# Handing a sum over states back from TensorE to GpSimd, and a new order of the first turns

## The chip, the cores and the metric

The kernel runs on one core of a Trainium2 chip. The metric is device time in microseconds (us) of one execution. The engines that matter are TensorE (PE, matmuls and transposes), VectorE (DVE), ScalarE (ACT), GpSimd (POOL) and SyncE (SP, which here only issues loads). Each engine runs its own instructions strictly in the order in which the program lists them; an instruction that has to wait for another engine holds up everything behind it on its own engine.

## The reference

A layer in the manner of Mamba, with a feed-forward part, and then a dense mixture of 8 experts. Tokens are x of shape (16, 256, 128): 16 sequences of 256 tokens, width 128, all in fp32. Cut to what matters:

```python
def layer(x):                         # one sequence after another, width 128
    xi, z = split(layernorm(x) @ in_proj_w.T)       # 256 inner channels each
    xc = silu(causal_conv(xi, 4 taps) + conv_b)
    dt, B, C = split(xc @ x_proj_w.T)               # 8, 16 and 16 columns
    dt = softplus(dt @ dt_proj_w.T + dt_proj_b)
    dA  = exp(dt * A)                               # for each of 16 states
    dBx = dt * B * xc
    h_t = dA_t * h_(t-1) + dBx_t                    # the scan over time
    y   = sum over the 16 states of h * C           # the "sum over states"
    y   = (y + D * xc) * silu(z)
    x   = x + y @ out_proj_w.T
    return x + relu(layernorm(x) @ w1.T + b1) @ w2.T + b2

x = layernorm(x + layer(x))
acc = 0
for e in range(8):                                  # every token through every expert
    acc += (silu(x @ Wg[e]) * (x @ Wu[e])) @ Wd[e]  # 128 -> 512 -> 128
out = layernorm(x + acc)
```

## The kernel before

The 16 sequences are cut into 8 groups of two, so a group has 512 tokens. Activations lie with channels on the 128 partitions and the 512 tokens along the row; the 256 inner channels are two halves. A group passes through these stages:

- `stage_a`: the loaded tokens `xt` (L209) are normalised (statistics `st_a` on DVE, L274; `rs`, `nb` on GpSimd, L283; four activations to `xh` on ScalarE, L291), transposed on PE (`pxn`, L298), scaled to `xn`, projected (`pi`), convolved (`hc`, `xc`), projected again (`pd`, `dbc`) and written to DRAM as `bc`, so that rows of B and C can be loaded back spread over all partitions. `dt` and `u` = dt * xc follow. `stage_gate` makes the gate `zg`.
- The scan. The 16 states of two halves make 32 steps per group (the text calls each of them a state; k counts them, so `hC_10` is step 10). Step k takes four to five instructions: `dA` = exp on ScalarE into one of three PSUM banks (L474, "decay"), `dBx` = B * u on GpSimd (L486, "inject"), the scan along time on DVE (L494), its product with C, `hC` (L497, on DVE, or on GpSimd where the scan wrote to SBUF, `hS`), and the addition to the running sum over states, `add_state`: `y` += `hC` on GpSimd (L523), or a matmul of `hC` with the identity into a PSUM bank `py` that PE keeps adding to (L521). Where a group's sum is on PE, the last step also adds `y` with a matmul (L527), and the product with the gate, `yt` (L536), runs on DVE; without it, `yt` runs on GpSimd.
- `stage_c`: `po` (16 matmuls out of `yt`, L551), `x1` on DVE, its norm (`st_b`, `ve_b` on DVE, `rs_b`, `nb_b` on GpSimd), `res` on GpSimd, `x1h`, `ph`, `h2`, four `pf` with their `r`, `pff`, `res` on DVE (L612), its norm (`ve_c`, `rs_c`), `x2` on ScalarE, the transposes `px` (L298 again) and the copy `x2T`, which feeds the experts.
- The experts: 32 slices a group (8 experts of 4 parts). A slice is `up` (`pg`, L641, and its Silu `h` on ScalarE, L643), `across` (`pu`, L650, and the product `h` = pu * h on DVE, L651) and `down` (`acc`, L667).
- `stage_e`: `ao`, `pao`, the last norm and the store.

Memory that sets the order: four rotating PSUM banks (`grab`, `give`, `take`) serve `pg`, `pu`, `py` and all the transposes and projections; B and C tiles of 512 KB hold four states each and have two buffers each, so the load of `B_12` (states 12 to 15) can't begin before the last `dBx` of `B_4` (`dBx_7`) has read it. All loads (tokens at L209, B and C at L463, expert weights at L251 to L253) go through SP's queue in program order.

The order of the instructions is written out by hand as strings of one-letter words. `PRE` is run once before the turns, `START` has one string for each of the first 18 turns, `TURN` has eight strings that repeat until the end. Each word does one thing if it can, and otherwise nothing:

- `d`, `i`, `s`, `a`: the next decay, inject, scan step, `add_state`; `p` is `s` with the product on GpSimd, `e` is `a` with the sum on PE
- `u`, `x`, `w`: the next up, across, down; `L`: loads of B and C whose conditions are met
- `A` (with `B`, `G`), `C`, `Z`: half a stage of `stage_a` (of convolutions, of gates), `stage_c`, `stage_e`; `P` prepares A
- `m` (`busy`): four transposes of the identity, filler, only while there are no experts; `S`, `E`: whether Silu and softplus may run now

The experts of group 0 begin once its `x2T` is there; until then PE has the filler, the projections and the sums. The tokens of group g+1 are asked for (`load_x`) at the top of a turn, and the turn's loads of B and C follow. In `add_state`, the condition on `on_pe` lets a group's first half of states start a sum on PE if more than two banks are free; once begun, any `e` goes on with it, and its bank is held until `yt`.

Of the kernel before, what the change touches and what calls it, by code (L numbers as in the profile page):

```python
# [12 lines left out]
P = 128  # L13
L = 256
DM = 128
NH = 2
NS = 16
# [15 lines left out]
NLATE = 4  # L33
# [15 lines left out]


PRE = (
# [4 lines left out]
)  # L56
START = (
# [44 lines left out]
)  # L102
TURN = (
# [26 lines left out]
def kernel(  # L130
# [25 lines left out]
    nc = tc.nc  # L156
# [15 lines left out]
    def bank(tag, name, bufs=1, w=TB):  # L172
        return ps.tile([P, TB], FP, tag=tag, bufs=bufs, name=name)[:, :w]


    free = list(range(NB))
    owner = {}

    def grab(name, w=TB):
        owner[name] = free.pop(0)  # L180
        return bank(f"b{owner[name]}", name, w=w)

    def give(name):
        free.append(owner.pop(name))
# [4 lines left out]
    def wides(tag, name, bufs, n, w):  # L189
        t = act.tile([P, n * TB], FP, tag=tag, bufs=bufs, name=name)  # L190
        return t[:, : n * w].rearrange("p (n w) -> p n w", n=n)
# [21 lines left out]
    ident = const.tile([P, P], FP, tag="ident", name="ident")  # L213
# [103 lines left out]
    def launch(kind, stage):  # L317

        next(stage)
        running[kind].append(stage)  # L320
# [178 lines left out]
    def sums(g, h):  # L499

        n = 1 if NH * W[g] <= TB else NH
        c = h * W[g] if n == 1 else 0
        return f"py{g}_{h if n > 1 else 0}", slice(c, c + W[g])

    def add_state(t, on_pe):

        g, k = scans[t]
        s = state[g]
        n, h = divmod(k, NH)
        hC = s.pop(("hC", k))  # L510
        y = s["y", h]
        last = n == NS - 1
        name, cols = sums(g, h)
        if on_pe and not (name in owner or (n < NS // 2 and len(free) > 2)):
            on_pe = False
        if on_pe or (last and ("sum", h) in s):
            first = name not in owner
            if first:
                s["py", name] = grab(name)
            s["sum", h] = s["py", name][:, cols]  # L520
            nc.tensor.matmul(s["sum", h], lhsT=ident, rhs=hC, start=first, stop=False, skip_group_check=True)  # L521
        else:
            nc.gpsimd.tensor_tensor(y, y, hC, ALU.add)  # L523
        if last:
            assert s["gated"] >= h
            if ("sum", h) in s:
                nc.tensor.matmul(  # L527
                    s["sum", h], lhsT=ident, rhs=y, start=False,
                    stop=h == NH - 1 or sums(g, NH - 1)[0] != name, skip_group_check=True,
                )  # L530
                y = s["sum", h]
            if h == 0:
                s["yt"] = wides("yt", f"yt{g}", 1, NH, W[g])

            engine = nc.vector if y is not s["y", h] else nc.gpsimd
            engine.tensor_tensor(s["yt"][:, h, :], y, s["zg"][:, h, :], ALU.mult)  # L536
            if name in owner and (h == NH - 1 or sums(g, NH - 1)[0] != name):
                give(name)
            if h == NH - 1:
                launch("C", stage_c(g))  # L540
# [91 lines left out]
    def parts(g, j):  # L632

        n = TB // W[g]
        return [divmod(j * n + i, NF) + (slice(i * W[g], (i + 1) * W[g]),) for i in range(n)]
# [18 lines left out]
    def down(g, j):  # L654
        s = state[g]
        if j == 0:

            n = NTAIL if g == NG - 1 else 1
            s["acc"] = [bank("dA" if i else "acc", f"acc{g}_{i}", ND if i else 1, W[g] // n) for i in range(n)]
        last = g == NG - 1  # L660
        late = last and j >= NJ[g] - NLATE
        if late and j < NJ[g] - 1:
            return
        todo = [p + (s.pop(("h", i)),) for i in range(j - NLATE + 1 if late else j, j + 1) for p in parts(g, i)]
        for part, acc in enumerate(s["acc"]):
            for e, f, cols, h in todo:
                nc.tensor.matmul(  # L667
                    acc, lhsT=wd[:, e, f, :], rhs=h[:, cols][:, bass.ts(part, acc.shape[1])],
                    start=(e == 0 and f == 0), stop=(e == NE - 1 and f == NF - 1),
                )  # L670
# [55 lines left out]
    def add_next(on_pe=False):  # L726
        g, k = scans[min(at["a"], len(scans) - 1)]
        if at["a"] < at["s"] and (
            k // NH < NS - 1 or state[g].get("gated", -1) >= k % NH and not running["C"]
        ):  # L730
            add_state(at["a"], on_pe)
            at["a"] += 1

    def step_next(pool=False):
        t = at["s"]
        if ready(t) and t < at["a"] + BUFS:
            if at["d"] == t:
                decay_next()
            if at["i"] == t:
                inject_next()  # L740
            if at["C"] * NL <= t:
                load_next("C")
            if min(at["d"], at["i"], at["C"] * NL) > t:
                step(t, pool)
                at["s"] += 1
# [21 lines left out]
    def silu(on):  # L767
        silus[0] = on or not experts

    def busy():  # L770
# [8 lines left out]
        L=loads, s=step_next, a=add_next, i=inject_next, d=decay_next, u=rise, x=cross, w=lower,  # L779
        S=lambda: silu(True), E=lambda: silu(False), m=busy,  # L780
        p=lambda: step_next(True), e=lambda: add_next(True),
# [10 lines left out]
    while at["w"] < sum(NJ) or any(running.values()):  # L792
# [3 lines left out]
        g, k = scans[min(at["a"], len(scans) - 1)]  # L796
# [56 lines left out]
```

## Time and profile before

| | us |
|---|---|
| Median of 3 runs | 934.35 (933.2 to 934.37) |
| The profiled execution's own time | 933.03 |
| Its span, first to last instruction | 930.9 |
| Busy in it: PE | 882.6 (95%) |
| DVE | 712.4 (77%) |
| ACT | 711.9 (76%) |
| POOL | 718.8 (77%) |

The mean granted TensorE clock is 0.979 of full speed. By stretches of the span, busy us of each engine, the granted clock, and the share of the DMA engines in use:

| Stretch | PE | DVE | ACT | POOL | Clock | DMA |
|---|---|---|---|---|---|---|
| 0 to 40 | 27.8 | 19.2 | 27.9 | 15.8 | 0.91 | 0.68 |
| 40 to 80 | 30.2 | 38.3 | 20.0 | 37.3 | 0.83 | 0.60 |
| 80 to 120 | 33.2 | 35.7 | 21.1 | 38.3 | 0.91 | 0.39 |
| 120 to 160 | 34.9 | 21.7 | 33.6 | 38.3 | 0.91 | 0.20 |
| 160 to 200 | 40.0 | 28.2 | 34.1 | 36.2 | 1.00 | 0.27 |
| 200 to 300 | 98.1 | 84.2 | 90.6 | 92.3 | 1.00 | 0.25 |
| 300 to 700 | 395.9 | 354.6 | 359.7 | 355.6 | 1.00 | 0.26 |

Mean durations of the large groups of instructions:

| Instruction | Line | ns | Count |
|---|---|---|---|
| `dBx` on POOL | L486 | 1275 | 256 |
| `y` on POOL | L523 | 1275 | 223 |
| `hC` on POOL | L497 | 1271 | 27 |
| scan on DVE | L494 | 1221 | 229 |
| `hC` on DVE | L497 | 691 | 229 |
| `h` product on DVE | L651 | 684 | 256 |
| `dA` on ACT | L474 | 685 | 256 |
| Silu `h` on ACT | L643 | 597 | 256 |
| table load on ACT | L474, L643 | 1283 | 91 and 90 |
| sum on PE | L521 | 695 | 66 rows |

How to read it: a PE, DVE, ACT or POOL row of the profile gives start and duration in us, engine, source line, operation, and out<-in; what stands in square brackets behind it is the idle time of the engine just before and what ended it. An fp32 matmul of 128x512 shows as two rows, so 33 sums are 66 rows. SPq is SP's DMA queue, and its rows are the moments at which a load is issued. A load of `xt` (256 KB) lands 4.4 us after its issue by the median of the eight.

### The profile page before, as it was taken

To read this page: it belongs to the slowest core of one execution; us is meant where nothing else is said; L and a number is where in the kernel's file an instruction comes from. 1 tells how busy PE (TensorE), PEld (TensorE's weight loads), DVE (VectorE), ACT (ScalarE), POOL (GpSimd) and SP (SyncE) were. 2 spreads that over 40 slices of the span, in tenths; PEclk is the share of its full clock that TensorE was granted. 3 is DMA by queue.
4 is the path that set the end of the run, shared out by engine and by line. 5 is a ranking of instruction groups with operands and counts; after the bars stand their busy time and mean duration, and the time that the engine had idled before them with its cause. 6 is when DMAs were issued, how large, how long until landed. Compare 5 with 4: busy or idle time off the path is not lost. (4 is left out here: it accounts for less than half of the span.)

```text
span 930.9 us, 8897 instructions
## 1 busy us (share of the span) xinstructions
PE 882.6 (95%) x2520; PEld 424.5 (46%) x2520; DVE 712.4 (77%) x1142; ACT 711.9 (76%) x996; POOL 718.8 (77%) x639
## 2 busy tenths in 40 slices
PE   6778797999999999999999999999999999999996
PEld 2334543445444543445344543454444544455564
DVE  4599865676989889988988998988898899723222
ACT  5834588888899799989898889979998889533222
POOL 1799998998999897999799879999799979700000
PEclk9888899999999999999999999999999999999998
DMA  7573411131233221223322223221322222000000
GB/s 203 199 236 137 134 62 68 68 103 57 82 102 110 83 90 60 91 90 102 94 79 90 80 94 101 92 96 53 103 90 92 91 79 90 1 1 11 1 0 12
DMA packets 38129, 79.76 MB, mean 86 GB/s; under 512 B 5936, under 2 KB 19136, under 8 KB 38080
## 3 DMA queue, kind: packets, MB, share of 16 engines
q1 hardware_dynamic: 33456, 76.58, 24.7%
q10 hardware_dynamic: 4624, 2.62, 1.0%
q8 instruction: 20, 0.33, 0.1%
q14 instruction: 29, 0.24, 0.1%
HBM read 76.57 MB, written 2.62 MB: 85 GB/s over the span
## 5 line engine op out<-in xcount | busy, mean ns | idle before, releaser
L486 POOL TENSOR_TENSOR dBx<-B,u 128x512 f32<-128x512 f32 x256 | 320.5, 1275 | 0.0
L494 DVE TENSOR_TENSOR_SCAN dA<-dA,dBx 128x512 f32<-128x512 f32 x229 | 279.7, 1221 | 17.0 <-ACT dA L474 14.0
L523 POOL TENSOR_TENSOR y<-y,hC 128x512 f32<-128x512 f32 x223 | 279.4, 1275 | 0.7 <-DVE hC L497 0.4
L641 PE MATMUL pg<-x2T,wg 128*128 128x512 f32 x512 | 255.7, 601 | 7.3 <-ACT h L643 4.8
L650 PE MATMUL pu<-x2T,wu 128*128 128x512 f32 x512 | 250.8, 595 | 3.3 <-ACT h L643 3.3
L651 DVE TENSOR_TENSOR h<-pu,h 128x512 f32<-128x512 f32 x256 | 170.9, 684 | 107.8 <-PE pu L650 104.8
L667 PE MATMUL acc<-h,wd 128*128 128x512 f32 (+1 forms) x576 | 251.4, 546 | 0.1
L643 ACT ACTIVATE h<-pg 128x512 f32<-128x512 f32 x256 | 147.1, 597 | 114.5 <-PE pg L641 112.4
L474 ACT ACTIVATE dA<-dt,A 128x512 f32<-128x512 f32 x256 | 169.4, 685 | 39.7 <-DVE hC L497 34.3
L497 DVE TENSOR_TENSOR hC<-dA,C 128x512 f32<-128x512 f32 x229 | 158.3, 691 | 18.0 <-POOL y L523 3.5
L667 PEld LDWEIGHTS acc<-h,wd 128*128 128x128 f32 x576 | 107.7, 191 | 110.2 <-issue 100.8
L650 PEld LDWEIGHTS pu<-x2T,wu 128*128 128x128 f32 x512 | 95.7, 190 | 123.0 <-issue 89.9
L641 PEld LDWEIGHTS pg<-x2T,wg 128*128 128x128 f32 x512 | 94.5, 191 | 123.2 <-issue 83.4
L474 ACT ACT_TABLE_LOAD x91 | 116.8, 1283 | 2.4 <-ACT x L291 0.5
L643 ACT ACT_TABLE_LOAD x90 | 115.5, 1283 | 3.3 <-ACT dbc L377 1.8
L283 POOL TENSOR_TENSOR rs_e<-ve_e,mhalf 128x4 f32<-128x4 f32 (+1 forms) x9 | 8.5, 945 | 123.4 <-DVE ve_e L281 123.4
L521 PE MATMUL py<-hC,ident 128*128 128x512 f32 x66 | 39.0, 695 | 9.8 <-DVE hC L497 6.0
L402 POOL TENSOR_TENSOR u<-dt,xc 128x512 f32<-128x512 f32 x15 | 19.5, 1302 | 30.0 <-ACT dt L397 30.0
L494 DVE TENSOR_TENSOR_SCAN hS<-dA,dBx 128x512 f32<-128x512 f32 x27 | 32.3, 1211 | 11.5 <-POOL hC L497 6.5
L443 DVE SCALAR_TENSOR_TENSOR hc<-pi,cw,hc 128x510 f32<-128x510 f32 (+2 forms) x48 | 35.5, 744 | 5.2 <-ACT hc L436 4.1
L497 POOL TENSOR_TENSOR hC<-hS,C 128x512 f32<-128x512 f32 x27 | 34.2, 1271 | 5.4 <-issue 3.2
L585 PEld LDWEIGHTS pff<-w,r 128*128 128x128 f32 x256 | 31.7, 194 | 9.4 <-issue 6.6
(90 smaller groups left out, 612.9 us busy)
## 6 DMA issues: line engine op xcount, KB each, us to landing
B<-bc SPq DMA_DIRECT2D x64, 512.0 KB, 3.8
C<-bc SPq DMA_DIRECT2D x64, 512.0 KB, 4.5
xt<-in_x_dram SPq DMA_DIRECT2D x8, 256.0 KB, 4.4
wg<-in_Wg_dram SPq DMA_DIRECT2D x8, 256.0 KB, 5.1
wu<-in_Wu_dram SPq DMA_DIRECT2D x8, 256.0 KB, 5.4
wd<-in_Wd_dram SPq DMA_DIRECT2D x8, 256.0 KB, 5.9
out_dram<-x ACTq DMA_DIRECT2D x7, 256.0 KB, 4.2
bc<-dbc ACTq DMA_DIRECT2D x8, 64.0 KB, 2.2
```

Source lines behind the costliest of these rows:

```text
L443: nc.vector.scalar_tensor_tensor(hv[:, :, k:], pv[:, :, : L - k], cw[:, h, KC - 1 - k : KC - k], hv[:, :, k:], ALU.mult, ALU.add,)
L474: nc.scalar.activation(s["dA", k], s["dt"][:, h, :], AF.Exp, scale=A_sb[:, h, n : n + 1])
L486: nc.gpsimd.tensor_tensor(s["dBx", k], s["B", k // NL][:, n % NC, :], s["u"][:, h, :], ALU.mult)
L494: nc.vector.tensor_tensor_scan(to, dA, s.pop(("dBx", k)), 0.0, ALU.mult, ALU.add)
L497: engine.tensor_tensor(hC, to, s["C", k // NL][:, k // NH % NC, :], ALU.mult)
L521: nc.tensor.matmul(s["sum", h], lhsT=ident, rhs=hC, start=first, stop=False, skip_group_check=True)
L523: nc.gpsimd.tensor_tensor(y, y, hC, ALU.add)
L641: nc.tensor.matmul(pg[:, cols], lhsT=wg[:, e, bass.ts(f, P)], rhs=s["x2T"], start=True, stop=True)
L643: nc.scalar.activation(s["h", j], pg, AF.Silu)
L650: nc.tensor.matmul(pu[:, cols], lhsT=wu[:, e, bass.ts(f, P)], rhs=s["x2T"], start=True, stop=True)
L651: nc.vector.tensor_mul(s["h", j], pu, s["h", j])
L667: nc.tensor.matmul(acc, lhsT=wd[:, e, f, :], rhs=h[:, cols][:, bass.ts(part, acc.shape[1])], start=(e == 0 and f == 0), stop=(e == NE - 1 ...
```

## The change

Three things are edited.

In `add_state`, a sum that a group has begun on PE may now be handed back. If the next `add_state` of the same half is called without PE (`a`, not `e`), it is not the last state, the group is not group 0 and the group's bank is held, then PE adds the running `y` to the bank with one more matmul against the identity, ScalarE copies the bank to `y`, the bank is given back, and the state itself is added on GpSimd as usual. `s["own", h]` notes it, and keeps that half from starting a sum on PE again. In the program that results, PE sums two of group 1's 32 states, `hC_1` and `hC_10`, and hands each back at once. Over the whole program PE's own sums of states (L521) go from 33 to 29, the matmuls of `y` at the last state from 3 to 2, and two matmuls and two copies are new; of the `hC` products, 17 are on GpSimd and 239 on DVE, where it was 27 and 229; the sums `y` on GpSimd are 227 for 223, `yt` 14 for 13.

In `down`, the products `h` are read and no longer removed from the table of names; the instructions are the same.

All the words of `PRE` and `START` are new (the strings of 18 turns, below only their beginnings); `TURN` stays. With them, among the loads on SP, the tokens of group 3 stand behind the load of `B_12` of group 2, where they stood before it.

```diff
 PRE = (
-    "L A B A G A L B A G B A A B G m G G A P L L B A A B B L B B "
...
+    "d B A G A B A B A B L A A B A G P B G B A L G P P i B A B A "
...
 )
 START = (
-    "C i C L L Z m e e a L d C Z p s C s A Z m L s m A s Z i s i "
-    "s e",
...
+    "A A L a s s C s A d C s s s p m a L L e Z e",
...
 )
...
         name, cols = sums(g, h)
-        if on_pe and not (name in owner or (n < NS // 2 and len(free) > 2)):
+        if on_pe and not (name in owner or (n < NS // 2 and len(free) > 2 and ("own", h) not in s)):
             on_pe = False
+        if not on_pe and not last and g > 0 and name in owner:
+
+            nc.tensor.matmul(s["sum", h], lhsT=ident, rhs=y, start=False, stop=True, skip_group_check=True)
+            nc.scalar.copy(y, s.pop(("sum", h)))
+            s["own", h] = True
+            give(name)
         if on_pe or (last and ("sum", h) in s):
...
-        todo = [p + (s.pop(("h", i)),) for i in range(j - NLATE + 1 if late else j, j + 1) for p in parts(g, i)]
+        some = range(j - NLATE + 1 if late else j, j + 1)
+        todo = [p + (s["h", i],) for i in some for p in parts(g, i)]
```

86 rows, old and new, of tables (PRE, START) are left out of this document.

## The prediction

> **What bounds the kernel now.** I read the page's engine shares and slices first, then PE's waits, then single engines in order of time around the second group.
>
> ```profile
> PE 882.6 (95%) x2520; PEld 424.5 (46%) x2520; DVE 712.4 (77%) x1142; ACT 711.9 (76%) x996; POOL 718.8 (77%) x639
> ...
> PE   6778797999999999999999999999999999999996
> ...
> POOL 1799998998999897999799879999799979700000
> ```
>
> PE (second row, 23.3 us a slice) is full from slice 7 on; before that it mostly runs filler (`busy`). So the time is: the start of the experts, the PE work behind it, and PE's waits there. GpSimd is as full as PE in slices 1 to 34; while the second group (group 1) is scanned, both bind.
>
> ```profile
> 121.61 2.99 PE L641 MATMUL pg<-x2T,wg 128*128 128x512 f32 x4
> ...
> 200.36 2.28 PE L551 MATMUL po<-outw,yt 128*128 128x128 f32 x16
> ...
> 227.84 0.60 PE L298 MATMUL px<-ident,x 128*128 128x128 f32 x4
> ```
>
> Experts start at 121.61; `po` of group 1 starts at 200.36, its `px` (the transposes whose copy is the next experts' input) at 227.84. From 121.6 to 200.4 PE has 81 matmuls of 128x512 at 0.86 (two rows each; four rows stand 1.72 apart), 69.7, in 78.8 us: 9.1 lost. From 200.4 to 227.8 it loses nothing.
>
> ```profile
> 199.49 1.27 POOL L536 TENSOR_TENSOR yt<-y,zg 128x512 f32<-128x512 f32 x1
> ...
> 204.91 1.02 POOL L283 TENSOR_TENSOR rs_b<-ve_b,mhalf 128x4 f32<-128x4 f32 x1 [0.47 <-DVE ve_b L281]
> ...
> 220.83 1.01 POOL L283 TENSOR_TENSOR rs_c<-ve_c,mhalf 128x4 f32<-128x4 f32 x1 [3.30 <-DVE ve_c L281]
> ```
>
> GpSimd finishes group 1's `yt` at 200.76, just as PE comes to `po`. Behind it lies slack: GpSimd waits 3.30, and DVE 5.90:
>
> ```profile
> 211.18 0.85 DVE L274 BATCH_NORM_STATS2 st_a<-xt 128x6 f32<-128x128 f32 x4
> ...
> 218.60 0.69 DVE L612 TENSOR_TENSOR res<-pff,res 128x512 f32<-128x512 f32 x1 [5.90 <-PE pff L585]
> ...
> 196.94 0.43 SPq L209 DMA_DIRECT2D xt<-in_x_dram x1
> ...
> 215.07 0.32 SPq L463 DMA_DIRECT2D B<-bc  x1
> ```
>
> The last two rows: group 3's tokens are asked for at 196.94, long before `st_a` reads them, and before the load of group 2's `B_12` at 215.07, which has to wait until GpSimd has read `B_4` for the last time (`dBx_7`).
>
> **The change, part by part.** Times are in us of the span; "order" is that of the changed program's instructions on each engine. Pitches, from rows that stand back to back in time: GpSimd 1.24 (five `dBx` in 6.16, nine in 11.10), a state on DVE (scan and `hC`) 1.93 (60.39, 62.32, 64.24), a scan alone 1.15 (two in 2.33), an `h` product 0.64 (two in 1.28), a matmul 0.86, a table load and the activation behind it 1.29 (137.94 to 139.23).
>
> *The handover.* Of group 1's 32 states two pass over PE (`hC_1`, `hC_10`), each followed by one matmul of `y` and one ScalarE copy out of PSUM: 4 x 0.86 on PE, of which two lie before the experts, beside filler. Before, 7 of group 1's sum matmuls lay behind the start of the experts, now 2: 5 x 0.86 = 4.3 of PE work leaves. The copy does not occur in the trace; the nearest rows, `x2T` (0.578) and `ao` (0.585), bound it; 0.58, hidden once behind `dA_11` and once between two Silus. The other edit (`s["h", i]` read, not popped) issues the same instructions: nothing.
>
> *GpSimd and DVE over the whole kernel.* `hC` on GpSimd 27 to 17, `y` 223 to 227, `yt` 13 to 14: -5 x 1.24 there; DVE takes ten `hC` more at 0.69 and loses one `yt`. One table load fewer on ScalarE, -1.28 (its row on the page).
>
> [...]
>
> *Start of the scan.* Group 1's four normalising activations (1.63) now stand ahead of group 0's `xn`, which covers a wait of 0.57: +1.0. A gate (0.6) and `dt` of group 1 (0.67), less one gate activation, stand ahead of the first decay: first scan at 35.2 for 33.1, +2.1.
>
> *Group 0.* Up to the second `yt`, DVE now has 27 states of 1.93 (scan and `hC`) and 6 scans of 1.15, where it had 28 and 5; with two `yt` of 0.64: 60.3 for 60.8. Then two states instead of one stand on DVE ahead of `x1`: `x1` at 99.3 for 95.8, +3.5. From there to the first expert it was 25.8; the `r` activations are less interrupted, and `x2T` now waits behind two `hc`: 24.9. Experts start at 124.2, +2.6.
>
> *Group 1's scan.* GpSimd from its first `dBx` to group 1's last `yt` has 134 instructions for 137: 158.9 busy for 162.7. Before, it idled 8.8 on the way (2.18, 0.44, 0.52, 0.68, 0.65, 0.44, 3.17, 0.72). The 3.17 goes back to PE, which had three banks left with `py` held and waited twice for a Silu (2.28 and 2.42); now the bank is back after one matmul. I take 4.9 idle: from 32.1 the last `yt` ends at 195.9, against 200.8. PE is there at 194.3 and has lost less than before. So far the change is 4.8 ahead.
>
> *From `po` to `px`: where it goes.* DVE had 3 scans and 4 `h` products between `ve_b` and `res`; now it has 7 states (5 x 1.93, 2 x 1.14), 7 products (0.64) and group 3's statistics (2.1): 18.5 without a gap, where it took 13.9 with 5.9 of slack. `ve_b` ends at 199.8, `res` at 218.4 at best, against 218.6: nearly all the lead is gone. PE, in order, now has `pxn` in front of `pg_30`, behind `xh`, behind four decays (three banks), the last of which waits for DVE's scan 7: `px` at 227.2 at best.
>
> *The queue.* In SP's order the load of `xt` for group 3 now stands behind that of `B_12`. `B_12` waits for `dBx_7` on GpSimd, the sixth instruction of 1.24 behind `rs_b`/`nb_b` (199.9 to 201.1): 208.5. `xt` is asked for at 208.85 and lands 3.0 to 5.8 later, median 4.4: 213.2. DVE comes to `st_a` at 199.8 + 0.62 + 1.93 + 4 x 0.62 + 2 x 1.93 = 208.7 and stands 4.5 (3.1 to 5.9). That this is a real wait the trace shows at the first groups, where the load stands behind `C_8`:
>
> ```profile
> 101.34 0.43 SPq L209 DMA_DIRECT2D xt<-in_x_dram  x1
> ...
> 105.75 0.87 DVE L274 BATCH_NORM_STATS2 st_a<-xt 128x6 f32<-128x128 f32 x4 [2.97 <-DMA xt<-in_x_dram]
> ```
>
> Queued behind `st_a` on DVE are scans 4 to 7 and `res`; behind those, ScalarE's `dA_7` to `dA_10`, two Silus, `xh`; behind `xh`, PE's `pxn`. PE is at `pxn` at 219.0 and can go on at 227.0: 8 idle. `px` then stands at 232.4, +4.6.
>
> *The clock.* After a gap of that length PE starts slow. Nearest rows:
>
> ```profile
> 99.90 1.63 PE L298 MATMUL ph<-ident,x1h 128*128 128x128 f32 x4 [4.14 <-ACT x1h L291]
> ...
> 102.39 3.78 PE L595 MATMUL pf<-h,w 128*128 128x512 f32 x4
> ...
> 153.70 1.43 PE L650 MATMUL pu<-x2T,wu 128*128 128x512 f32 x2 [2.42 <-ACT h L643]
> ```
>
> After 4.14 idle four rows took 3.78 (1.88 warm) and the transposes 1.0 more; after 2.42 two rows took 0.4 more. Between 0.4 and 2.9; I take 2.0, nearer the long gap.
>
> *Behind `px`.* `pxn` already lies in front: -0.4. Matmuls left are the same (after `px` 31/29/28 of up, across and down are done; before 31/30/27). DVE and GpSimd have 9 instructions fewer each until group 2's `px`; the waits of before between 230 and 290 (0.70 + 0.34 + 0.34 + 0.17 + 0.28 = 1.8) may shrink: -1.2, between -1.8 and 0. From there both programs repeat the same turns.
>
> Sum: +4.6 + 2.0 - 0.4 - 1.2 = **+5.0**. The profiled execution took 933.03 (span 930.9 and 2.1 around it), the median of the runs is 934.35: 938.0 and 939.4; I say 938.7.
>
> **Rivals.**
> *The load is hidden after all* (not slower). `st_a` waits less if DVE is late itself or GpSimd passes `dBx_7` early; for it, DVE's stretch is 18.5 of unbroken work. Then `px` comes at 227.2: -0.6 - 0.4 - 1.2 = -2.2, and some 0.7 for hops between engines that I left out: 932.5. Against it: both times hang on the same `ve_b`, so lateness moves them together; it decides only if the load stands under 1 us.
> In this case PE idles 3.5 at `pxn`, between the two clock rows. [...]
>
> *The lead at `po` is kept* (not slower). If PE's fewer matmuls and the earlier `yt` carry through, -4.8 + 0.9 (one product fewer was done by `po`) - 0.4 = -4.3: 930.0. For it: PE's 9.1 of loss in group 1's scan. Against it: DVE's 18.5.
>
> *GpSimd slips too* (slower). My walk leaves GpSimd 0.3 to 1.1 of margin at `hC_17`, `hC_24` and `hC_28` behind DVE's scans; a wait there like the old 3.17, ScalarE's 13 table pairs being in series with it, adds 3 to 4.5 on top: 942.
>
> *It does not do what it says*: two states of 32 on PE is hardly a sum begun there; the order decides. That is in the forecast.
>
> **How the numbers follow.** Forecast (slower by 2 to 7) 0.50; with GpSimd slipping 0.14; load hidden 0.22; lead kept 0.14. A measurement tells about 0.2% (1.9 us) from no change. Faster: the last case and a third of the hidden one, 0.20. Same: the rest of that and the forecast's low edge, 0.16. Slower 0.64. The forecast's own range is 935.5 to 941.5 (stall 3.1 to 5.9, clock 0.4 to 2.9). The range over cases: 931 to 943.5.
>
> **What would show it.** In the changed profile: first scan near 35, `pg` at 124, group 1's `yt` near 196; SP's `xt` some 0.4 behind `B_12`; DVE waiting 3 to 6 at `st_a` for a DMA; PE waiting about 8 at `pxn` for `xh`, with a lower clock behind it; `px` near 234. I am wrong if `st_a` finds its data, or if `yt` of group 1 ends after 199.

## The result and the profile after

The changed kernel takes 939.83 us (median of 3 runs, 939.39 to 939.96) where the kernel before took 934.35; the ratio is 1.0062, 95% interval 1.0039 to 1.0084. It is slower by 5.5 us; 938.7 was forecast. Later, beside the experiments, the same kernel took 941.31 against 933.48 (1.0075, 1.0062 to 1.0088). The profiled execution took 939.96, its span is 938.2 (930.9 before).

From the page of the changed kernel: the engines' busy times, and the slices of PE, GpSimd and PE's granted clock.

```profile
PE 873.5 (93%) x2514; PEld 417.0 (44%) x2514; DVE 717.6 (76%) x1151; ACT 709.6 (76%) x997; POOL 713.4 (76%) x634
...
PE   6577789987999999999999999999999999999996
...
POOL 1699999996799878999699969998799979700000
PEclk9799999998999999999999999999999999999998
```

PE is busy for 9 us less and GpSimd for 5 less, in a longer span. PE's row has an 8 and a 7 in the ninth and tenth slice (188 to 235 us), where the kernel before had nines, and its clock is 8 in the tenth. That place in time, from the timelines of the engines (start, duration, engine, line, what is written out of what; in brackets the idle time before and what ended it):

```profile
122.24 1.12 PE L642 MATMUL pg<-x2T,wg 128*128 128x512 f32 x2 [1.65 <-ACT x2T L626]
...
193.20 1.26 POOL L537 TENSOR_TENSOR yt<-y,zg 128x512 f32<-128x512 f32 x1
...
194.52 2.64 PE L552 MATMUL po<-outw,yt 128*128 128x128 f32 x14 [2.31 <-POOL yt L537]
...
199.43 1.02 POOL L278 TENSOR_TENSOR rs_b<-ve_b,mhalf 128x4 f32<-128x4 f32 x1 [1.29 <-DVE ve_b L276]
...
208.62 0.43 SPq L204 DMA_DIRECT2D xt<-in_x_dram  x1
...
213.75 0.88 DVE L269 BATCH_NORM_STATS2 st_a<-xt 128x6 f32<-128x128 f32 x4 [4.76 <-DMA xt<-in_x_dram]
...
217.08 0.69 ACT L469 ACTIVATE dA<-dt,A 128x512 f32<-128x512 f32 x1 [3.06 <-DVE hC L492]
...
222.25 0.68 DVE L613 TENSOR_TENSOR res<-pff,res 128x512 f32<-128x512 f32 x1
...
224.75 1.64 ACT L286 ACTIVATE xh<-xt,nb_a,rs_a 128x128 f32<-128x128 f32 x4
225.30 1.62 PE L293 MATMUL pxn<-ident,xh 128*128 128x128 f32 x4 [3.50 <-ACT xh L286]
226.71 1.92 PE L642 MATMUL pg<-x2T,wg 128*128 128x512 f32 x2
228.42 1.55 PE L669 MATMUL acc<-h,wd 128*128 128x512 f32 x2
...
232.38 0.60 PE L293 MATMUL px<-ident,x 128*128 128x128 f32 x4
```

Group 1's `yt` ends at 194.46, 6.3 earlier than before. Then the tokens of group 3 are asked for at 208.62, behind `B_12`; DVE stands 4.76 for them; the decays behind its scans are late (3.06); `xh` stands behind the decays, and PE stands 3.50 for `xh`. The two matmuls behind it take 1.71 at a clock of 0.50 and 1.38 at 0.62 to the next start, where one at 1.00 takes 0.86. `px` is 4.5 later than before. A comparison that stopped here would seem to have the whole result. It would be wrong, as the starts of `px` in all groups show:

| Start of `px`, group | 0 | 1 | 2 | 3 | 4 | 5 | 6 | 7 | end of span |
|---|---|---|---|---|---|---|---|---|---|
| Before | 119.30 | 227.84 | 330.77 | 433.26 | 535.17 | 637.08 | 738.99 | 832.39 | 930.9 |
| After | 119.49 | 232.38 | 331.35 | 434.42 | 537.19 | 640.32 | 742.99 | 837.02 | 938.2 |
| Difference | 0.19 | 4.54 | 0.58 | 1.16 | 2.02 | 3.24 | 4.00 | 4.63 | 7.3 |

The 4.5 shrink to 0.6 by group 2, and then grow by 0.6 to 1.2 in each group of turns whose strings were not changed. Counted from the word lists: when the repeating turns begin (turn 18), the kernel before has begun 32, 30 and 28 slices of the experts (up, across, down), the changed one 31, 29 and 27. (It is also one `dBx` and one sum ahead there; e2 below keeps that lead and has the pace of before.) The profiles agree: at `px` of group 2 PE has run 63, 62 and 59 before, 62, 61 and 58 after, and one less in every later group too. One slice is three matmuls, 3 x 0.86 = 2.6 us of PE. So of the 4.54, 2.6 are gone by group 2 only because that work is still to be done, and the remaining 1.4 are gained on the way; the slice is paid at the end (4.63 to 7.3). The new cost is the 4.05 between group 2 and group 7.

GpSimd's timeline in group 4 shows where it comes from. Before:

```profile
449.68 1.28 POOL L486 TENSOR_TENSOR dBx<-B,u 128x512 f32<-128x512 f32 x1
456.12 1.02 POOL L283 TENSOR_TENSOR rs_e<-ve_e,mhalf 128x4 f32<-128x4 f32 x1 [5.16 <-DVE ve_e L281]
...
468.89 1.27 POOL L402 TENSOR_TENSOR u<-dt,xc 128x512 f32<-128x512 f32 x1 [1.67 <-ACT dt L397]
```

After, with PE's row of the same group:

```profile
457.28 1.02 POOL L278 TENSOR_TENSOR rs_e<-ve_e,mhalf 128x4 f32<-128x4 f32 x1 [7.61 <-DVE ve_e L276]
...
458.53 1.28 POOL L524 TENSOR_TENSOR y<-y,hC 128x512 f32<-128x512 f32 x1
459.77 1.27 POOL L481 TENSOR_TENSOR dBx<-B,u 128x512 f32<-128x512 f32 x1
...
510.79 1.83 PE L552 MATMUL po<-outw,yt 128*128 128x128 f32 x14 [1.07 <-POOL yt L537]
```

With the slices one later, the steps of `stage_e` fall on other `Z` words, and `rs_e` is issued two GpSimd instructions earlier. The `y` and `dBx` that used to run ahead of it, while `ve_e` was not there, now stand behind it: GpSimd waits 7.61 and not 5.16, the wait of 1.67 for `dt` goes, and 0.78 is left. The 0.78 is also what a group loses in e5 below, where only the slice is missing (102.69 from `px` to `px`, 101.91 before). `po` of groups 3 to 6 waits 1.03 to 1.35 for `yt`, before 0.27 to 0.30.

### The profile page after: what moved, and what is told of

It is laid out like the page before. It is cut to its first block, busy times and chain, and to the rows that moved or that the text cites. A ratio compares the mean times of both kernels' runs of the same rounds, so it can differ in the third digit from the quotient of the medians.

```text
span 938.2 us, 8910 instructions
## 1 busy us (share of the span) xinstructions
PE 873.5 (93%) x2514; PEld 417.0 (44%) x2514; DVE 717.6 (76%) x1151; ACT 709.6 (76%) x997; POOL 713.4 (76%) x634
## 5 line engine op out<-in xcount | busy, mean ns | idle before, releaser
L489 DVE TENSOR_TENSOR_SCAN dA<-dA,dBx 128x512 f32<-128x512 f32 x239 | 292.0, 1222 | 17.7 <-ACT dA L469 11.8
L524 POOL TENSOR_TENSOR y<-y,hC 128x512 f32<-128x512 f32 x227 | 284.9, 1280 | 1.5 <-DVE hC L492 1.2
L652 DVE TENSOR_TENSOR h<-pu,h 128x512 f32<-128x512 f32 x256 | 171.0, 684 | 110.2 <-PE pu L651 107.5
L492 DVE TENSOR_TENSOR hC<-dA,C 128x512 f32<-128x512 f32 x239 | 165.3, 692 | 18.1 <-POOL y L524 3.0
L522 PE MATMUL py<-hC,ident 128*128 128x512 f32 x58 | 32.0, 653 | 17.9 <-DVE hC L492 14.4
L600 ACT ACTIVATE r<-pf,fb 128x512 f32<-128x512 f32 x32 | 20.7, 684 | 15.1 <-PE pf L596 15.1
L586 PE MATMUL pff<-w,r 128*128 128x128 f32 x256 | 31.5, 275 | 0.0
```

What stands on the lines that cost most here:

```text
L489: nc.vector.tensor_tensor_scan(to, dA, s.pop(("dBx", k)), 0.0, ALU.mult, ALU.add)
L492: engine.tensor_tensor(hC, to, s["C", k // NL][:, k // NH % NC, :], ALU.mult)
L586: nc.tensor.matmul(po[:, bass.ts(c, P)], lhsT=r[:, f, bass.ts(c, P)], rhs=w2[:, f, :], start=start and c == 0, stop=stop and c == W[g] // ...
L652: nc.vector.tensor_mul(s["h", j], pu, s["h", j])
```

## The experiments

All times are medians, each against the kernel before on the same chip. "px 2 to 7" is the time from `px` of group 2 to that of group 7, which no start-up reaches: 501.6 before, 505.7 after.

| Run | Kernel | us | Before | Ratio (95%) | px of group 1 | px 2 to 7 |
|---|---|---|---|---|---|---|
| e12 | after, again | 941.31 | 933.48 | 1.0075 (1.0062 to 1.0088) | 231.87 | 505.4 |
| e1 | after, tokens ahead | 934.81 | 933.12 | 1.0010 (0.9999 to 1.0021) | 224.66 | 505.5 |
| e2 | after, a slice more | 937.85 | 933.12 | 1.0051 (1.0038 to 1.0064) | 236.46 | 502.2 |
| e3 | after, both | 930.90 | 933.12 | 0.9977 (0.9965 to 0.9990) | 229.22 | 501.9 |
| e4 | before, tokens late | 936.58 | 933.12 | 1.0038 (1.0025 to 1.0050) | 231.16 | 501.2 |
| e5 | before, a slice less | 938.36 | 933.89 | 1.0044 (1.0032 to 1.0056) | 226.68 | 504.7 |
| e6 | before, a slice more | 945.06 | 933.89 | 1.0122 (1.0108 to 1.0136) | 227.23 | 513.0 |
| e7 | after, no sum on PE | 942.47 | 933.89 | 1.0087 (1.0072 to 1.0101) | 235.17 | 505.4 |
| e8 | e1, slice ahead of `po` | 929.41 | 933.89 | 0.9950 (0.9935 to 0.9964) | 226.66 | 501.4 |
| e9 | e8, `pxn` later | 926.07 | 933.70 | 0.9924 (0.9911 to 0.9938) | 224.13 | 501.3 |
| e10 | before, handover | 940.83 | 933.70 | 1.0083 (1.0069 to 1.0097) | 238.53 | 501.4 |
| e11 | after, `rs_e` later | 939.98 | 933.48 | 1.0066 (1.0053 to 1.0080) | 232.31 | 502.1 |

**e1, the tokens ahead.**

```diff
+        if turn == 16:
+            load_x(3)
         if g + 1 < NG and g + 1 not in x_tiles:
```

> The changed kernel, with group 3's tokens asked for one turn earlier, so that their load stands ahead of those of B_8 and B_12 on SP's queue; nothing else moves. Theory A (two causes: the load behind B_12 costs the wait at st_a and PE's wait at pxn; one slice fewer begun at the end of the hand-written start costs some 0.8 us in each repeating group): st_a waits for no DMA, px of group 1 near 227.5 where the changed kernel has 232.4, po of groups 2 to 6 still waits 1.0 to 1.4 for yt, time 3 to 5 us less than the changed kernel, 935 to 937. Rival B (the stall only takes the place of another wait, GpSimd or the four decays holding ScalarE anyway): px above 231 and less than 1.5 us gained, 938.5 or more.

Timelines of DVE and PE in this kernel:

```profile
207.41 0.86 DVE L269 BATCH_NORM_STATS2 st_a<-xt 128x6 f32<-128x128 f32 x4
...
215.93 0.68 DVE L613 TENSOR_TENSOR res<-pff,res 128x512 f32<-128x512 f32 x1
...
219.04 1.48 PE L293 MATMUL pxn<-ident,xh 128*128 128x128 f32 x4 [1.07 <-ACT xh L286]
...
224.66 0.60 PE L293 MATMUL px<-ident,x 128*128 128x128 f32 x4
```

`st_a` waits for nothing, `res` starts 6.3 earlier than in the changed kernel, `px` 7.7 earlier, more than the 4.9 expected; the repeating turns lose as before (505.5). Not all of the 7.7 is the load's. `po` waits 2.30 for `yt` here too, but PE's clock stays at 1.00 behind it, where it fell to 0.67 and 0.50 in the changed kernel's execution; that makes 1.6, which is there before the load plays a part. The rest is the load's: PE waits 4.8 less at `pg` and `pxn`, and the clock behind them (1.00 here, 0.50 to 0.62 there) is worth 1.4. In the medians, each against the kernel before, the move is worth 5 to 6 us (1.0010 for 1.0062 and 1.0075).

**e2, one slice more at the end of the start.**

```diff
-    "p d x C C i w a u Z u C i A C C A i a L u L u Z w x m w i",
+    "p d x C C i w a u Z u C i A C C A i a L u L u Z w x m w i u x w",
```

> The changed kernel with one more u, x and w word at the end of the last hand-written turn, so that the repeating turns begin with 32, 30 and 28 slices up, across and down, as in the kernel before, and not with 31, 29 and 27. Theory A: the wait at st_a stays (4.8), but the copies ao come earlier in ScalarE's order, po of groups 3 to 6 waits 0.3 for yt and not 1.1, px to px is 101.9 to 102.2 and not 102.7 to 103.1, and the time is 3 to 4.5 us less than the changed kernel, 935.5 to 937. Rival C (the repeating turns lose because they are entered late or with their banks in another order, not by the slice): px to px stays at 102.8, time 939 to 941.

`po` waits 0.28 to 0.30 in groups 3 to 6, from one group's `px` to the next it takes 101.9, and px 2 to 7 falls by 3.5: the repeating turns are as before. The time fell less than expected (ratio 1.0051 against 1.0075 of e12): in this execution PE's clock is 0.50 from 194.4 to 201.2, from the end of the same wait at `po` on, and `px` of group 1 is 4.1 later, of which 2.6 is the slice.

**e3, both.** The edits of e1 and e2 together.

> Both edits at once. Theory A: they add up, 6.5 to 9.5 us less than the changed kernel, 930.5 to 933, so 1 to 4 us less than the kernel before. Rival B or C: no more than the better of the two alone.

930.90, faster than before (0.9977). The two causes add up within the noise; without them nothing of the 5.5 to 7.8 is left.

**e4, the tokens late in the kernel before.** `B_12` is loaded at the top of turn 17, ahead of the tokens:

```diff
+        if turn == 17:
+            load_next("B")
         if g + 1 < NG and g + 1 not in x_tiles:
```

> The kernel before with group 3's tokens asked for behind the load of B_12; nothing else moves. Theory A: the load is issued near 215.5, lands near 220, st_a waits 7 to 9, uses up the 5.9 of slack before res and holds xh and the Silus behind it, px of group 1 is 3 to 5 us later with a slow clock, and the time is 3 to 6 us more than before, 937.5 to 940. Rival B: the slack of 5.9 takes up most of it, less than 1.5 us more.

SP's queue and DVE in this kernel:

```profile
215.63 0.43 SPq L209 DMA_DIRECT2D xt<-in_x_dram  x1
...
220.78 0.87 DVE L274 BATCH_NORM_STATS2 st_a<-xt 128x6 f32<-128x128 f32 x4 [9.34 <-DMA xt<-in_x_dram]
...
222.12 0.68 DVE L612 TENSOR_TENSOR res<-pff,res 128x512 f32<-128x512 f32 x1
```

DVE stands 9.34, and `res` comes 3.5 later: of 9.34 the old slack before `res` took up 5.9. The time rises by 3.5. A wait twice as long as the changed kernel's costs little more than half as much, because DVE had time there. In the new order it has none: in e1 DVE stands idle for no more than 0.10 at a time from `ve_b` to `res`.

**e5 and e6, a slice less and a slice more in the kernel before.** The last `u`, `x` and `w` of `START` are left out (e5), or `x w u` is added at its end (e6).

```diff
-    "i d a Z p u w x C A d C L d C i s m E d a C Z L w a i L L A "
-    "u L A",
+    "i d a Z p u w C A d C L d C i s m E d a C Z L a i L L A "
+    "L A",
```

> The kernel before with the last u, x and w words of the hand-written start left out, so that the repeating turns begin with 31, 29 and 27 slices, as in the changed kernel, and not 32, 30 and 28. Everything else is as before. Theory A (the slice alone makes the repeating turns lose): po of groups 3 to 6 waits 1.0 to 1.4 for yt, where it waits 0.3; px of group 2 to px of group 7 takes 505 to 506 us, where it takes 501.6; time 3 to 4.5 us more than before. Rival C (entry time or order of banks): 501.6 stays, less than 1 us more.

> The kernel before with one more u, x and w word at the end of the hand-written start (33, 31, 29). If the loss grows with every slice that ao comes later, it shrinks further here: po waits nothing, px of group 2 to px of group 7 takes 499.5 to 501, time 0.5 to 2 us less. If the 0.3 left is only the hop from GpSimd to PE, or another engine binds: 501 to 502, time within 1 us of before.

e5 makes the loss by itself: `po` waits 1.01 to 1.02, `rs_e` 7.61, px 2 to 7 takes 504.7, the time rises by 4.5, without any of the new words or the handover. GpSimd in e5, group 4, in the same order as in the changed kernel:

```profile
456.35 1.02 POOL L283 TENSOR_TENSOR rs_e<-ve_e,mhalf 128x4 f32<-128x4 f32 x1 [7.61 <-DVE ve_e L281]
...
457.60 1.27 POOL L523 TENSOR_TENSOR y<-y,hC 128x512 f32<-128x512 f32 x1
458.83 1.26 POOL L486 TENSOR_TENSOR dBx<-B,u 128x512 f32<-128x512 f32 x1
```

e6 went against its expectation: 11.2 us more. In PE's timeline of this kernel (group 4):

```profile
439.63 1.12 PE L641 MATMUL pg<-x2T,wg 128*128 128x512 f32 x2 [1.09 <-ACT x2T L625]
...
450.01 1.12 PE L667 MATMUL acc<-h,wd 128*128 128x512 f32 x2 [0.68 <-ACT ao L680]
```

A slice of the next group is now due right behind its `px`, so the first `pg` waits for `x2T`, and the first `acc` for `ao` to empty the bank. GpSimd's `rs_e` waits 7.21. The strings of the repeating turns fit one count of slices at their start; one less costs 0.8 a group, one more 2.3 (104.23 for 101.91).

**e7, no sum on PE in group 1.**

```diff
-        if on_pe and not (name in owner or ...
+        if on_pe and (g == 1 or not (name in owner or ...
```

> The changed kernel with group 1's sum never begun on PE: hC_1 and hC_10 are added on GpSimd, and the two handing matmuls and two copies fall away; order of the words unchanged. Theory A with GpSimd binding group 1's scan: 2 x 1.24 more there, of which at most 0.6 goes into its waits; the last yt 1.9 to 2.5 us later than 194.5, px of group 1 2 to 4 later, time 2 to 4 us more than the changed kernel, 941.5 to 944. Rival D (two states are too few to matter): within 1 us of the changed kernel.

GpSimd makes the two sums at 107.5 and 142.3, 1.24 each, but about 1.0 of that goes into waits that it had in the changed kernel (0.25 for `ve_a`, 0.17 for `ve_c`, 0.61 at 149.88). So the last `yt` ends at 195.61, 1.15 after the changed kernel's and not 1.9 to 2.5. `po` waits 3.29 and runs at a clock of 0.50 (195.6 to 199.0), `px` is 2.8 later. The experts start later too (123.38 for 122.24), with PE's clock at 0.50 from 117.1 to 123.9 in this execution. In time the interval overlaps that of e12, so what the handover is worth in the new order stays open.

**e8 and e9, filling PE's waits.** e8 has e1's edit and the slice ahead of group 1's `po`; e9 moves the `A` word that issues `pxn` to the end of its turn.

```diff
-    "s u m w i C C m e Z a x i w L C d Z i w S Z C S C i S u x L "
+    "s u m w i C C m e Z a u x i w L x w C d Z i w S Z C S C i S u x L "
...
-    "p d x C C i w a u Z u C i A C C A i a L u L u Z w x m w i",
+    "p d x C C i w a u Z u C i A C C i a L u L u Z w x m w i A",
```

> The changed kernel with the tokens of group 3 asked for a turn earlier, and the slice more not at the end of the start but ahead of po of group 1, where PE waits 2.3 for yt and its clock drops in some executions. If that wait and the clock behind it are what is left: 1.5 to 3 us less than with the slice at the end (930.9), 928 to 929.5, and less spread between runs. Rival: the slice's Silu and product are in the way of dA and of x1, and it gains nothing, 930 to 933.

> As e8, and the transposes pxn of group 3 moved behind five of PE's matmuls (one up, one across, three down less one), by moving one A word of the last hand-written turn to its end. PE then has 3.4 us of work in the 2.2 that it waits for xh; but ScalarE's x2 stands behind xn, which waits for pxn, so that px can come at 225.4 at best where it comes at 226.7. 0.8 to 2 us less than e8, 927.5 to 928.6. Rival: the wait turns up again at px and nothing is gained, 929 to 930.

e8 takes 929.41, as expected, and e9 926.07, the fastest of all (0.9924) and 3.3 less than e8 where 0.8 to 2 was expected. In e8 `po` of group 1 no longer waits; in e9 `pxn` finds `xh`, where it waited 2.21 in e8, and `px` is 2.5 earlier. PE in e9:

```profile
222.28 0.60 PE L293 MATMUL pxn<-ident,xh 128*128 128x128 f32 x4
...
224.13 1.48 PE L293 MATMUL px<-ident,x 128*128 128x128 f32 x4 [0.39 <-ACT x L286]
```

**e10, the handover alone, in the old order.** The new condition and the five lines of `add_state` in the kernel before. PE then hands back `hC_2` and `hC_7` of group 1 and sums no other of its states.

> The kernel before, its old order of words, with the handover alone: PE then sums hC_2 and hC_7 of group 1 and hands each back, where it summed seven states (hC_2 to hC_30) and kept the bank to the end. GpSimd gets five y and one yt more, 6 x 1.24 = 7.4, and loses its wait of 3.17. If GpSimd binds group 1's scan: the last yt 3 to 5 us later (204 to 206), time 3 to 6 us more than before, 937 to 940. Rival: PE's bank and its 4 matmuls fewer are worth more (its waits of 2.28 and 2.42 go), px earlier, 930 to 933.

PE's timeline:

```profile
207.04 0.80 PE L557 MATMUL po<-outw,yt 128*128 128x128 f32 x2 [7.38 <-POOL yt L542]
209.60 3.36 PE L557 MATMUL po<-outw,yt 128*128 128x128 f32 x14 [1.76 <-POOL yt L542]
```

The last `yt` ends at 209.55, 8.8 later than before. Of this, 1.6 are there at the first scan (34.70 for 33.09), where the handover has no part: in this execution, 2.1 slower than the median, PE's clock is 0.50 from 22.4 to 29.3. Another 1.9 come up to the start of the experts, and 5.3 behind it; PE waits 9.1 at `po`. The time rises by 7.1, more than expected. By itself the handover moves five sums and a product to GpSimd, the engine that is full. The new order of the words has to make up for that, and does: its last `yt` is 6.3 earlier than before.

**e11, `rs_e` back behind its two neighbours.** In the last norm the two GpSimd instructions are issued one `Z` word after DVE's:

```diff
-        scale = norm_stats(x2, f"e{g}_{part}")
+        scales = norm_stats(x2, f"e{g}_{part}", later=True)
         yield
+        scale = scales()
```

> The changed kernel with one thing moved: rs_e and nb_e of the last norm are issued one Z word later, which puts them behind the two GpSimd instructions (y of hC_11, dBx_17) that stood ahead of them before the change; PE, DVE and ScalarE have the same order as in the changed kernel, the slice stays missing. If the slice costs the repeating turns only through this place on GpSimd: rs_e waits 5.2 and not 7.6, po of groups 3 to 6 waits 0.3, px of group 2 to px of group 7 takes 501.6 to 502.5 where the changed kernel takes 505.7, time 3 to 4 us less than the changed kernel. Rival (the later ao and its waits on ScalarE and PE cost it): 505 to 506, and no more than 1 us less.

> The changed kernel itself beside e11 and the kernel before on one chip, as the time that the others are measured against: 4.5 to 6.5 us more than before.

GpSimd in e11, group 4:

```profile
458.44 1.02 POOL L279 TENSOR_TENSOR rs_e<-ve_e,mhalf 128x4 f32<-128x4 f32 x1 [5.14 <-DVE ve_e L276]
...
471.22 1.27 POOL L400 TENSOR_TENSOR u<-dt,xc 128x512 f32<-128x512 f32 x1 [1.66 <-ACT dt L395]
```

The repeating turns are cured, as expected, with the slice still missing: waits of 5.14 and 1.66 as before, `po` 0.28 to 0.29, px 2 to 7 at 502.1. The time is only 1.3 less than e12's, a miss: between `px` of groups 1 and 2 it loses 2.0. There GpSimd had no idle time to give (`rs_e` of group 0 waits 0.41 in e12); two instructions later, it makes ScalarE wait 1.76 for `nb_e`, and PE waits 1.32 behind that.

## Why the prediction was right, and where it was not

The direction and the time were right, 938.7 against 939.83, and the mechanism that the forecast was built on is there: the load behind `B_12` (issued 208.62, I had 208.85), `st_a` waiting 4.76 (4.5, range 3.1 to 5.9), `pxn` waiting for `xh` behind the decays, a slow clock behind that (0.50 to 229.47). e1 and e4 show that the load's place does it. That the sum came out right is in part luck: it had `px` of group 1 2.0 too late (234.4 for 232.38) and left out the 4.05 that the repeating turns lose. Over the profiled spans it forecast +5.0 where +7.3 was measured; the medians are only 5.5 apart, as the execution profiled before was 1.3 faster than its median.

- *First scan, experts, last `yt`.* Predicted 35.2, 124.2, 195.9; measured 34.60, 122.24, 194.46. The start was costed too dear: group 0's `x1` came at 97.95, not 99.3. GpSimd's idle time up to `yt` was 4.0 for the 4.9 I took. `po` waited 2.31 for `yt`; I had PE there 1.6 ahead.
- *"Nearly all the lead is gone"* failed. Without the late load `px` comes at 224.66 (e1), not at 227.2 "at best": 3.2 of the lead are kept, 1.6 less where the clock falls behind `po`. 1.4 of the difference is the earlier `yt`, the rest is DVE's stretch from `ve_b` to `res`: 17.3 (198.67 to 215.93) for 18.5, mostly group 3's statistics, 1.37 for the 2.1 I added up from their durations. For the load I had 5.2 (232.4 for 227.2) and 2.0 for the clock behind it; between e1 and the changed kernel these are 4.8 and 1.4.
- *PE's idle time of 8* was 5.6, 3.50 at `pxn` and 2.06 at the `pg` ahead of it, which waited for DVE too. *The clock's 2.0*, all of it behind `pxn`, was 1.4 there. Another 1.6, for `po` and the first matmul behind it, had no term in the sum. One of the rows it was taken from was misread: the transposes that took 1.0 more behind the wait of 4.14 (99.90) start 0.39 apart, as ScalarE's `x1h` do; in e1 and e9 four transposes fed so take 1.48 at a clock of 1.00. Of the 1.0 the clock made 0.15.
- *"Behind px": -0.4 and -1.2.* Measured to group 2's `px`, with the slice's 2.6 counted in: -1.4.
- *"From there both programs repeat the same turns"* is the step that failed most. The strings are the same, the instructions are not: I counted the matmuls left behind `px` of group 1 (equal, 88 and 88), but not the slices begun where the repeating strings take over, one less. That costs 4.05 in the profile; e5 shows it alone (+4.5), e2 and e3 cure it.

Of the rivals, "the lead is kept" had the right view of the order and the wrong one of the load: with the load out of the way (e1) the time is 1.7 above before, its interval just reaching no change, because of the slice: e3 has neither and is faster by 2.2. "The load is hidden after all" did not come: `st_a` waited 4.76. "GpSimd slips too" did not come: its only wait between 120 and `yt` is 0.61. "The order decides" is only partly right: in the old order the handover alone costs 7.1 (e10), as it leaves GpSimd five sums more; the new order makes up for that.

## What to carry to other kernels

Where an order is written out by hand and then repeats, compare the two programs at the moment when the repeating part takes over: how many steps of each pipeline are done, not only what remains. A loss of 0.8 a round is hard to see in PE's waits (1.0 to 1.35 at `po` for 0.3), and shows at once in a table of one event per round.

The load that was moved in the queue took over the wait of what now stands ahead of it (`xt` issued at 208.62 behind `B_12`, at 196.94 ahead of it). Where a load is moved, look for the first instruction that needs it, and ask whether that engine had slack there (here 5.9 before, none after).

## What the runs showed of the hardware

Behind a wait of 2.3 us on PE the clock fell to 0.50 in one execution and stayed at 1.00 in another. The windows of two kernels around group 1's `po`, with the same wait (columns: stretch, its length, busy PE, weight loads, DVE, ACT, POOL, granted clock, DMA share, GB/s). The changed kernel:

```profile
194.50:196.90 2.40, 2.38 (x14) 2.38 (x15) 0.00 (x0) 2.37 (x3) 2.40 (x3) 0.67 0.00 0
196.90:198.70 1.80, 1.80 (x5) 0.77 (x4) 1.47 (x5) 0.54 (x1) 1.25 (x2) 0.50 0.39 143
```

e1:

```profile
194.60:196.30 1.70, 1.65 (x14) 1.65 (x15) 0.00 (x0) 1.67 (x3) 1.70 (x2) 1.00 0.00 0
196.30:198.00 1.70, 1.70 (x6) 0.78 (x5) 1.45 (x5) 1.69 (x2) 1.70 (x2) 1.00 0.00 0
```

Both had waited for `yt`, 2.31 and 2.30; the first went on at 0.67 and 0.50, the second at 1.00. The profiles also give the times at which the clock changed. In the changed kernel it is 0.50 from 195.34 to 198.75, which is 3.41 us, and from 222.64 to 229.47, twice that. In the 3.41 us ahead of each of these PE was busy for 1.1. In e1 PE was busy for as little of the 3.41 us that end with its wait (3.41 less 2.30), and the clock stayed at 1.00. What decides it is not shown.

e1's 12 runs go from 931.76 to 935.89, those near 932 with a mean clock of 0.989 and those near 935 to 936 with 0.984 (one with 0.987). That this wait decides between them is not shown: only one of the 12 has a profile. e9, which leaves neither of the two long waits, stays within 925.12 and 927.40 in five runs.

Four transposes that take 1.48 where others take 0.60 are not a sign of a slow clock by themselves: in e9 `px` took 1.48 with the clock at 1.00 from 224.1 to 225.4, as four activations of ScalarE fed them; such activations start 0.38 to 0.40 apart in the profiles (`x1h` before, from 99.35; `xh` after, from 224.75).
